# An RNN layer with a gated residual: the input product x Wx issued in two row tiles of 64 partitions in place of the undivided array

## The chip, the cores and the metric

The kernel runs on one core of one Trainium2 chip. The metric is the device time of one execution in microseconds (us), as the median of several runs; lower is better. TensorE's granted clock in the profile of before is 1.000 of full speed.

## The reference, cut to what matters

x is 64 sequences of 256 steps of 1024 numbers, in float32. A first layer adds to x the states of a recurrent network, a second adds a gated copy:

```
N, T, D = 64, 256, 1024
xW = einsum('ntd,dh->nth', x, Wx) + b
for t in range(T):                       # each step needs the one before
    h = tanh(h @ Wh + xW[:, t])          # h starts as cond (64 x 1024)
    out[:, t] = h
x = x + out
gate = sigmoid(silu(cond @ W1.T + b1) @ W2.T + b2)
x = x + inverse_haar(gate * haar(x))     # the gate is one number per sequence and column
```

Since the gate does not depend on the step, the second layer is a multiplication of x by 1 + gate, and the kernel does it so (`factor`).

## The kernel before, in words

The steps are taken in 128 pairs: the 64 sequences of two steps make 128 rows, the tile that TensorE takes as weights. Two products fill the time.

**The product of h, once per step.** h Wh is made in seven products of half the size (Strassen's scheme, `strassen_product`, line 192). Each is 4 blocks times 4 column tiles of 32 (`tile_position=(0, q * R)`, line 204), in plain float32; each matmul is two instructions in the profile, so a product is 32 instructions of line 197. Seven products make a step. Between products ScalarE (ACT) and VectorE (DVE) add, take tanh and transpose; the banks `main0` and `main1` serve here as `m5` and `m7` (line 748).

**The product x Wx, once per pair.** To keep precision with one-pass matmuls (type fp32r), x is split into three parts and Wx too: x0 is the high bits (`high_bits` on DVE, then `cast` on ACT, line 309), x1 the low rest (`low`, line 297), x2 a difference (`difference`, line 302). x2 times the third part of Wx goes into the accumulators `mixed`; x1 and x0 times their parts go into `main`. The 1024 output columns are two halves `h` of 512, one accumulator bank each (`mixed0`, `mixed1`, `main0`, `main1`), and the 1024 of contraction are 8 blocks `k` of 128 rows. So a pair takes 3 x 2 x 8 = 48 matmuls, 128 rows x 128 weight columns, 512 moving columns (`x_matmul`, line 274).

For pairs 7 to 127 these 48 come in `whole` (line 333) in one piece: `mixed` for both halves, then x1 into `main`, then x0. Pairs 1 to 6, in the first twelve steps, use `block`, `first` and `second`.

`take_mixed` (line 317) copies `mixed` out on ACT, half by half, into `sum` and adds the bias on GpSimd (POOL). `finish_half(h)` (line 374) adds `main[h]` to it on DVE. `store` and `reload` (384, 388) carry `sum` through DRAM on SP's queue to the layout of the step, `xw`, which `put_part` (line 611) copies into the accumulators of the coming step.

**Order.** From step 12 on the program orders all engines by hand. Steps go in groups of three (`M = 3`), and after each group comes `beside_x` (line 654): one `whole`, or, where the coming group needs the pair at once (`many`), two with nothing between them on TensorE. In it DVE prepares the next pair's x2 and x1 (`prepare`, line 677) before `finish_half(0)` and `finish_half(1)`; ACT does `take_mixed`, then three `put_part`, then the `cast` of the next pair (line 703, or at the first step of the next group, line 776); POOL multiplies finished x by `factor` (`scale`) and adds the bias. The tiles `high`, `x0`, `x1`, `x2` and `sum` exist once each, and so do the four banks: each is written again only after its last reader.

Of the kernel before, what the change touches and what calls it, by code (L numbers as in the profile page):

```python
# [53 lines left out]
F32 = mybir.dt.float32  # L54
# [7 lines left out]
P = 128  # L62
R = 32
Q = P // R
B = D // P
# [6 lines left out]
M = 3  # L72
NP = T // S
HALF = 512
HIGH = -(1 << 12)
UP = float(1 << 12)
DOWN = 1.0 / UP
# [8 lines left out]
def tile_cond_resid(  # L86
# [14 lines left out]
    nc = tc.nc  # L101
    const = ctx.enter_context(tc.tile_pool(name="const", bufs=1))
# [18 lines left out]
    def high_bits(v, name: str):  # L121
        t = split.tile([P, D], I32, tag="high", name=name)
        nc.vector.tensor_scalar(out=t, in0=v.bitcast(I32), scalar1=HIGH, scalar2=None, op0=ALU.bitwise_and)
        return t[:].bitcast(F32)
# [111 lines left out]
    def put(xw, t: int):  # L236

        acc = bank("acc", f"acc{t}")
        nc.scalar.copy(acc, flat(xw))
        return acc  # L240

    def h_product(acc, a: dict, t: int):

        m16, m57 = (bank(f"m{i}", f"m{i}_{t}") for i in (16, 57))
        m16, m5, m7 = m16[:, :E], m57[:, :E], m57[:, E : 2 * E]
        part = [acc[:, i * E : (i + 1) * E] for i in range(3)]
        y = sums.tile([P, 4, E], F32, tag="y", name=f"y{t}")
        u = sums.tile([P, E], F32, tag="u", name=f"u{t}")
        strassen_product(m16, a[1], 1, True)
        nc.scalar.copy(y[:, 0], m16)  # L250

        strassen_product(part[0], a[2], 2) if t != S else None
        strassen_product(m5, a[5], 5, True)
        strassen_product(m16, a[6], 6)
        nc.scalar.copy(u, m16)
        strassen_product(m7, a[7], 7)
        strassen_product(part[0], a[2], 2) if t == S else None
        if t == 1:
            for k in range(B - 2, B):
                gate_block(k)  # L260
        nc.vector.tensor_add(
            y[:, 1:3], m57[:, : 2 * E].rearrange("p (i e) -> p i e", i=2), u[:].unsqueeze(1).broadcast_to((P, 2, E))
        )
        nc.vector.tensor_add(y[:, 3], m7, y[:, 1])
        strassen_product(part[2], a[4], 4)
        strassen_product(part[1], a[3], 3)
        h = work.tile([P, W], F32, tag="h", bufs=1, name=f"h{t}")
        nc.vector.tensor_add(h, acc, flat(y))
        return h

    def bank(tag: str, name: str):
        return one_pool.tile([P, HALF], F32, tag=tag, name=name)

    def x_matmul(acc, v, which: int, h: int, k: int, start=False, stop=False) -> None:

        nc.tensor.matmul(  # L276
            out=acc[h],
            lhsT=v[:, k * P : (k + 1) * P],
            rhs=wx_s[k][which][:, h * HALF : (h + 1) * HALF],
            start=start and k == 0,  # L280
            stop=stop and k == B - 1,
        )

    class XWork:
# [32 lines left out]
        def take_mixed(self) -> None:  # L317
            self.sum = split.tile([P, D], F32, tag="sum", name=f"sum_{self.i}")
            for h in range(2):
                s = self.sum[:, h * HALF : (h + 1) * HALF]  # L320
                nc.scalar.activation(s, self.mixed[h], AF.Copy, scale=-1.0)  # L321
                nc.gpsimd.tensor_add(s, s, b_row[:, h * HALF : (h + 1) * HALF])  # L322

# [9 lines left out]
        def whole(self) -> None:  # L333

            self.begin()
            for h in range(2):
                for k in range(B):
                    x_matmul(self.mixed, self.x2, 2, h, k, True, True)
            for h in range(2):
                for k in range(B):  # L340
                    x_matmul(self.main, self.x1, 1, h, k, start=True)
            for h in range(2):
                for k in range(B):
                    x_matmul(self.main, self.x0, 0, h, k, stop=True)

        def first(self) -> None:
            self.cast()
# [26 lines left out]
        def finish_half(self, h: int) -> None:  # L374
            v = self.sum[:, h * HALF : (h + 1) * HALF]
            nc.vector.scalar_tensor_tensor(  # L376
                out=v, in0=self.main[h], scalar=1.0 + DOWN, in1=v, op0=ALU.mult, op1=ALU.add
            )
# [40 lines left out]
    wx_s, wh_raw = [], []  # L419
# [15 lines left out]
    acc, acc1, gate_ps = bank("acc", "acc0"), bank("m57", "acc1_raw"), bank("gate", "gate_ps1")  # L435
# [57 lines left out]
    def x_step(t: int):  # L493
        x = pairs[t // S][:].rearrange("p (b s g m) -> p s g b m", b=B, s=S, g=G)
        return x[:, t % S]
# [7 lines left out]
    h = work.tile([P, W], F32, tag="h", bufs=1, name="h0")  # L503
# [4 lines left out]
    for t in range(ALONE):  # L508
# [3 lines left out]
        if t:  # L512
            h = h_product(acc, sides, t)
# [4 lines left out]
        if t == 0:  # L518
            acc = bank("acc", "acc1")
# [18 lines left out]
        elif s == 0:  # L538
            acc = put(xw[1], t + 1)
# [4 lines left out]
        if s == 1 and t + 1 < ALONE:  # L544
            now = later
            now.first()
            acc = put(xw_next[0], t + 1)
# [17 lines left out]
        if LATE <= t < LATE + B:  # L565
            k = t - LATE
# [44 lines left out]
    def put_part(t: int, j: int):  # L611

        part = bank(("acc", "m57", "gate")[j], f"acc{t}_{j}")[:, :E]
        nc.scalar.copy(part, xws[t // S][t % S][:, j])
        return part
# [100 lines left out]
    def kept_step() -> None:  # L716
# [4 lines left out]
        def at(v, n: int):  # L721
            return v[n // S].rearrange("p (b s n) -> p s b n", b=B, s=S)[:, n % S]
# [6 lines left out]
        if not odd:  # L729
# [3 lines left out]
            if n < S * len(kept):  # L733
                again.append(const.tile([P, W], F32, tag="spare", name=f"again{n}"))
                v = again[0][:].rearrange("p (b n) -> p b n", b=B)
                nc.sync.dma_start(out=v, in_=at(kept, n))

    accs = [put_part(ALONE, j) for j in range(3)]
    ends, factors, gaps = [], [], [0]
    later.cast()  # L740
# [2 lines left out]
    for t in range(ALONE, T):  # L743
# [7 lines left out]
        h = work.tile([P, W], F32, tag="h", bufs=1, name=f"h{t}")  # L751
# [35 lines left out]
        elif t > T - 4:  # L787

            v = x_step(t - 1)
# [76 lines left out]
```

## Time and profile before

| | |
|---|---|
| median of 3 runs | 3050.32 us (3049.7 to 3053.82) |
| span of the profiled execution, first to last instruction | 3054.6 us (no other time of this execution is recorded) |
| PE, TensorE's matmuls | 3039.8 us, 63862 instructions |
| PEld, its weight loads | 2716.7 us, 63862 |
| DVE | 1796.3 us |
| ACT | 864.0 us |
| POOL | 772.3 us |
| matmuls of x Wx (line 276) | 4064 into `main`, 2032 into `mixed` |

A line of the page's groups gives source line, engine, operation, output and inputs by the program's names, shapes and count; then busy time in us and the mean of one in ns; then the idle time of the engine before the group and what ended most of it. PE and PEld are two views of TensorE and overlap. Consecutive matmuls overlap as well, so the duration of one is longer than the time from one start to the next; a rate has to be read from starts. In the order of time, a row is a run of equal instructions: start in us, length in us, engine, line, group, count.

### The profile page before, as it was taken

The numbers are of one execution on the slowest core, as the hardware profiler recorded it, in microseconds if no ns is written. First come the engines' busy times: TensorE is split into PE (matmuls) and PEld (weight loads), VectorE is DVE, ScalarE is ACT, GpSimd is POOL, SyncE is SP. The second block draws the span as 40 slices with busy tenths as digits, with TensorE's granted clock in tenths as the row PEclk, the third lists the DMA queues.
The fourth block names the chain that finished last, engine by engine and source line by source line (L and its number), as shares of the span: only waits on it lengthen the run. The fifth ranks groups of instructions, "written<-read, shape, count | busy, mean of one in ns | idle before, by whom it ended". The sixth has DMA issues, their size and how long they took to land.

```text
span 3054.6 us, 141755 instructions
## 1 busy us (share of the span) xinstructions
PE 3039.8 (100%) x63862; PEld 2716.7 (89%) x63862; DVE 1796.3 (59%) x4928; ACT 864.0 (28%) x2641; POOL 772.3 (25%) x521
## 2 busy tenths in 40 slices
PE   9999999999999999999999999999999999999999
PEld 6888998888899988999888889888899988889998
DVE  8555555555555655556555555556556555555555
ACT  3222322222222222222222222222222222222222
POOL 2232222222222222222222222222222222222221
PEclk9999999999999999999999999999999999999999
DMA  7323222333322232222323222223222223332222
GB/s 263 125 98 98 92 92 96 106 103 102 114 91 86 85 100 98 86 86 86 102 96 104 93 86 85 86 88 98 97 86 85 85 97 96 103 100 85 86 85 82
DMA packets 164605, 300.40 MB, mean 98 GB/s; under 512 B 44192, under 2 KB 110496, under 8 KB 164000
## 3 DMA queue, kind: packets, MB, share of 16 engines
q1 hardware_dynamic: 163856, 290.81, 28.6%
q8 instruction: 501, 8.21, 1.1%
q14 instruction: 104, 0.85, 0.1%
q10 hardware_dynamic: 144, 0.52, 0.0%
HBM read 154.93 MB, written 136.31 MB: 95 GB/s over the span
## 4 chain that ended last, share of the span: by engine, by line
PE 99%; issue 0%; POOL 0%; DMA 0%; DVE 0%; SPq 0%; ACT 0%; DVEq 0%
PE main L276 30%; PE acc L197 22%; PE mixed L276 16%; PE m_h L197 14%; PE main_h L197 14%; PE m L197 1%; PE acc L214 0%; PE gate_ps L214 0%; POOL sum L322 0%; DMA wx<-wx 0%; PE acc_raw L214 0%; DVE x L300 0%; SPq L413 0%; ACT sum L321 0%; SPq L119 0%
## 5 line engine op out<-in xcount | busy, mean ns | idle before, releaser
L276 PE MATMUL main<-wx,x 128*128 128x512 f32 x4064 | 945.7, 389 | 0.4 <-DVE x L300 0.4
L276 PEld LDWEIGHTS main<-wx,x 128*128 128x128 f32 x4064 | 762.1, 188 | 161.2 <-issue 2.2
L501 POOL TENSOR_TENSOR x<-x,factor 128x512 f32<-128x512 f32 x242 | 312.0, 1289 | 1318.3 <-DVE x L619 931.5
L322 POOL TENSOR_TENSOR sum<-sum,b_row 128x512 f32<-128x512 f32 x254 | 421.0, 1667 | 849.0 <-ACT sum L321 840.5
L276 PE MATMUL mixed<-wx,x 128*128 128x512 f32 x2032 | 494.7, 395 | 0.0
L276 PEld LDWEIGHTS mixed<-wx,x 128*128 128x128 f32 x2032 | 374.9, 188 | 92.8 <-issue 17.1
L756 ACT ACTIVATE h<-h 128x128 f32<-128x128 f32 x976 | 275.7, 306 | 569.3 <-DVE h L780 376.6
L300 DVE TENSOR_TENSOR x<-x,x_high 128x1024 fp32r<-128x1024 f32 x127 | 178.7, 1407 | 265.5 <-PE main L276 265.5
L760 DVE STREAM_TRANSPOSE hT<-h 128x128 f32<-128x128 f32 x972 | 298.0, 307 | 38.5 <-ACT h L756 38.4
L376 DVE SCALAR_TENSOR_TENSOR sum<-main,sum 128x512 f32<-128x512 f32 x254 | 175.4, 691 | 205.2 <-PE main L276 179.8
L197 PE MATMUL acc<-wh,s 128*32 128x128 f32 x8160 | 283.7, 273 | 2.7 <-issue 2.4
L197 PE MATMUL acc<-wh,hT 128*32 128x128 f32 x8160 | 277.8, 273 | 0.7 <-issue 0.6
L197 PE MATMUL acc<-t,hT 128*32 128x128 f32 x8160 | 276.0, 273 | 1.0 <-issue 0.9
L197 PE MATMUL main_h<-wh,s 128*32 128x128 f32 x7808 | 269.9, 273 | 1.3 <-issue 1.1
L197 PE MATMUL main_h<-t,s 128*32 128x128 f32 x7808 | 269.9, 273 | 1.2 <-issue 0.9
L197 PE MATMUL m_h<-t,s 128*32 128x128 f32 x7808 | 269.7, 273 | 0.8 <-issue 0.6
L197 PE MATMUL m_h<-wh,hT 128*32 128x128 f32 x7808 | 263.7, 274 | 0.2
L305 DVE SCALAR_TENSOR_TENSOR x<-x_high,x 128x1024 fp32r<-128x1024 f32 x127 | 178.8, 1408 | 133.5 <-PE mixed L276 133.4
L321 ACT ACTIVATE sum<-mixed 128x512 f32<-128x512 f32 x254 | 146.9, 598 | 366.3 <-DMA sum_d<-sum 186.6
L197 PEld LDWEIGHTS acc<-wh,s 128*32 128x32 f32 x8160 | 237.5, 110 | 7.0 <-issue 7.0
L197 PEld LDWEIGHTS m_h<-wh,hT 128*32 128x32 f32 x7808 | 213.8, 110 | 30.1 <-issue 29.5
L197 PEld LDWEIGHTS acc<-wh,hT 128*32 128x32 f32 x8160 | 234.0, 110 | 3.7 <-issue 2.6
(81 smaller groups left out, 2751.3 us busy)
## 6 DMA issues: line engine op xcount, KB each, us to landing
x<-xT SPq DMA_DIRECT2D x127, 512.0 KB, 4.6
sum_d<-sum SPq DMA_DIRECT2D x127, 512.0 KB, 3.1
xw<-sum_d SPq DMA_DIRECT2D x1016, 64.0 KB, 2.0
yT<-x SPq DMA_DIRECT2D x122, 512.0 KB, 2.8
wh<-wh SPq DMA_DIRECT2D x8, 512.0 KB, 11.0
w<-w1T SPq DMA_DIRECT2D x8, 512.0 KB, 8.7
w<-w2T SPq DMA_DIRECT2D x8, 512.0 KB, 4.4
wx<-wx SPq DMA_DIRECT2D x7, 512.0 KB, 8.5
```

The costliest lines, as they stand in the source:

```text
L197: nc.tensor.matmul(out=out[q * R : (q + 1) * R], lhsT=a[:, k * R : (k + 1) * R], rhs=wh_s.sides[i][k][:, q], start=first and k == 0, stop= ...
L276: nc.tensor.matmul(out=acc[h], lhsT=v[:, k * P : (k + 1) * P], rhs=wx_s[k][which][:, h * HALF : (h + 1) * HALF], start=start and k == 0, s ...
L300: nc.vector.tensor_sub(self.x1, x, self.high)
L305: nc.vector.scalar_tensor_tensor(out=self.x2, in0=self.high, scalar=1.0 + DOWN, in1=pairs[i], op0=ALU.mult, op1=ALU.subtract)
L321: nc.scalar.activation(s, self.mixed[h], AF.Copy, scale=-1.0)
L322: nc.gpsimd.tensor_add(s, s, b_row[:, h * HALF : (h + 1) * HALF])
L376: nc.vector.scalar_tensor_tensor(out=v, in0=self.main[h], scalar=1.0 + DOWN, in1=v, op0=ALU.mult, op1=ALU.add)
L501: nc.gpsimd.tensor_mul(of_step(x, s), of_step(x, s), blocks(factor))
L756: nc.scalar.activation(quad(h, j), quad(h, j), AF.Tanh)
L760: nc.vector.transpose(quad(hT, j), quad(h, j))
```

## The change

`whole` issues the same sums in another cut. A matmul no longer covers the 128 rows of block k; it covers 64, and two such matmuls, one for the upper and one for the lower 64 rows (`r`), are issued one after the other at `tile_position=(0, 0)` and `(64, 0)`. At any time the two write different banks: in the first three passes (`turned = 0`; x2, x1, x0) row tile 0 works for half 0 and row tile 1 for half 1; in the last three, halves are exchanged, so that each bank has received both row tiles' parts at the end. A pass is 8 blocks x 2 = 16 matmuls with 512 moving columns; six passes make 96 matmuls with their weight loads where there were 48. After the first and the third pass ACT copies one element of `mixed[1]` or `main[1]` into a spare tile `turn`; the next write of row tile 0 into that bank, two passes or one pass later, waits for this reader.

```
         def whole(self) -> None:
 
             self.begin()
-            for h in range(2):
-                for k in range(B):
-                    x_matmul(self.mixed, self.x2, 2, h, k, True, True)
-            for h in range(2):
-                for k in range(B):
-                    x_matmul(self.main, self.x1, 1, h, k, start=True)
-            for h in range(2):
-                for k in range(B):
-                    x_matmul(self.main, self.x0, 0, h, k, stop=True)
+            for turned in range(2):
+                for acc, v, which in ((self.mixed, self.x2, 2), (self.main, self.x1, 1), (self.main, self.x0, 0)):
+                    for k in range(B):
+                        for r in range(2):
+                            h = r ^ turned
+                            rows = slice(r * HP, (r + 1) * HP)
+                            nc.tensor.matmul(
+                                out=acc[h],
+                                lhsT=v[rows, k * P : (k + 1) * P],
+                                rhs=wx_s[k][which][rows, h * HALF : (h + 1) * HALF],
+                                start=not turned and k == 0 and which > 0,
+                                stop=turned == 1 and k == B - 1 and which != 1,
+                                skip_group_check=True,
+                                tile_position=(r * HP, 0),
+                            )
+                    if not turned and which != 1:
+                        nc.scalar.copy(turn, acc[1][:1, :1])
...
+    turn = const.tile([1, 1], F32, tag="turn", name="turn")
```

`HP` is 64. Nothing else is changed; the other users of `x_matmul` stay.

More of the change, by code (lines that the diff above doesn't have):

```diff
@@ L74 @@
 HALF = 512
+HP = P // 2
 HIGH = -(1 << 12)
```

## The prediction

> **What bounds the kernel now.** I read the page from the chain of work downwards, since it says whose time the end is made of, then the costliest groups, then the order of time in one stage.
>
> ```profile
> span 3054.6 us, 141755 instructions
> ...
> PE 3039.8 (100%) x63862; PEld 2716.7 (89%) x63862; DVE 1796.3 (59%) x4928; ACT 864.0 (28%) x2641; POOL 772.3 (25%) x521
> ...
> PE 99%; issue 0%; POOL 0%; DMA 0%; DVE 0%; SPq 0%; ACT 0%; DVEq 0%
> ...
> L276 PE MATMUL main<-wx,x 128*128 128x512 f32 x4064 | 945.7, 389 | 0.4 <-DVE x L300 0.4
> L276 PEld LDWEIGHTS main<-wx,x 128*128 128x128 f32 x4064 | 762.1, 188 | 161.2 <-issue 2.2
> ...
> L276 PE MATMUL mixed<-wx,x 128*128 128x512 f32 x2032 | 494.7, 395 | 0.0
> ...
> L197 PEld LDWEIGHTS acc<-wh,s 128*32 128x32 f32 x8160 | 237.5, 110 | 7.0 <-issue 7.0
> ```
>
> The chain is TensorE and nothing else. The 6096 matmuls of x Wx (4064 + 2032, 48 for each of 127 pairs) keep it busy for 1440 us. Their idle time before is 0.4 us, so they wait for nobody. What an edit does here it does through the time between matmul starts. A weight load of 128 columns is shown as 188 ns, one of 32 columns (the products of h) as 110.
>
> The durations overlap, so a rate is read from starts. Next view: TensorE in order of time, over two pairs that follow each other (the stage in which `whole` runs twice) and the first products of h behind them. Columns: start us, duration of the merged run, then the group and its count.
>
> ```profile
> 1030.39 3.92 PE L276 MATMUL mixed<-wx,x 128*128 128x512 f32 x16
> 1034.15 7.42 PE L276 MATMUL main<-wx,x 128*128 128x512 f32 x32
> 1041.41 3.79 PE L276 MATMUL mixed<-wx,x 128*128 128x512 f32 x16
> 1045.04 7.42 PE L276 MATMUL main<-wx,x 128*128 128x512 f32 x32
> 1052.38 1.08 PE L197 MATMUL m_h<-wh,hT 128*32 128x128 f32 x32
> 1053.28 1.06 PE L197 MATMUL acc<-t,hT 128*32 128x128 f32 x32
> 1054.15 1.06 PE L197 MATMUL acc<-wh,hT 128*32 128x128 f32 x32
> ```
>
> From 1034.15 to 1041.41, 32 matmuls take 7.26 us: **226.9 ns each**; the 16 from 1041.41 take 3.63, again 226.9. The first 16 take 3.76, so entering from the products of h costs 0.13 us. A product of h, 32 instructions in four column tiles side by side, takes 0.87 us (1053.28 to 1054.15; 0.873 over the six that follow): 218.3 ns for eight. The start of the kernel has column tiles with 256 moving columns:
>
> ```profile
> 21.30 1.05 PE L214 MATMUL acc_raw<-wx,x 128*32 128x256 f32 x16
> 22.17 1.05 PE L214 MATMUL acc<-wx,x 128*32 128x256 f32 x16
> 23.03 1.05 PE L214 MATMUL acc_raw<-wx,x 128*32 128x256 f32 x16
> 23.89 7.09 PE L214 MATMUL acc<-wh,h0T 128*32 128x256 f32 x128
> ```
>
> 48 in 2.59 us: four side by side take **215.8 ns**. Their mean duration (379 to 413 by tile) is near the 389 of an x matmul, so one instruction of theirs is about as long as one of L276, yet a round of them returns in 216 where the undivided array needs 227. So 11 ns of each x matmul are a gap which rows with tiles side by side do not have.
>
> **The change, part by part.** *Matmuls.* In each of 121 `whole` calls (pairs 7 to 127; the first six go through `block`, `first` and `second`, untouched) 48 matmuls of 128 rows become 48 couples of 64 rows, with the same 512 columns and 128 weight columns per member. That makes 5808 couples, and 5808 more matmuls and weight loads. Each ns of couple time P is worth 5.81 us. No row shows row tiles. Bounds: P = 215.8 (the column tiles' round) gives (226.9 − 215.8) × 5.81 = −64.5 us; P = 453.8 (members one after the other) +1318 us. Between ends so far apart I go by the nearest rows, those with tiles side by side: 215.8 and, with twice as many weight columns in a round (8 × 32 = 256, just what a couple loads), 218.3. I take the middle, 217.1: 9.8 × 5.81 = **−56.9 us**.
>
> *Weight loads.* They double: 256 columns per couple instead of 128. In a product of h 256 columns are loaded in 218.3 ns beside the matmuls, so this load rate is shown to hide; 188 − 110 = 78 ns for 96 more columns is 0.81 ns per column, 208 for 256, also under 217. If the cover is gone, the second rival follows. The Trainium skill speaks against the change here (TensorE: Matmul & The Clock Gate, "LDWEIGHTS (loading the stationary operand)"): load time goes by columns, columns / 1.2 ns, and fewer rows save nothing. The row's slope (0.81) agrees; by the page a couple's loads make an estimated 213 ns, 4 under my P, and the sum would stand. The same page ("Wait — 56ns, not 53.3ns?") gives 215.7 ns from start to start for 512 columns once warm; the measured 226.9 disagrees, and by the page there would be no gap to win on the undivided array.
>
> *Entering and leaving.* `beside_x` runs 81 times (40 with two `whole`, 41 with one: 121). Entering costs 0.13 now; the first couple must load twice, at most 109 ns more (half of 218), or the entry could vanish. Bounds −10.5 to +8.8 us; I take half a load: **+4.4 us**.
>
> *Turn copies.* 242 ACT copies of one element. The smallest PSUM copies of the trace, 128x128, take 0.26 to 0.27 us (the `u` and `acc` copies), so at most 65 us on an engine that is 28% busy. TensorE waits for them: pass 4 for a copy of the end of pass 1, pass 5 for one of the end of pass 3. Slack: two passes (3.5 us) and one (1.7 us) against 0.2 us release and 0.27 us copy. Ahead of the copy on ACT stand tanh and `cast` (1.06), done 1.2 us into the second `whole`. Cost 0; behind the copies wait `take_mixed`, which is later anyway.
>
> *What moves.* `mixed` ends after pass 4, not after the first third; `main0` and `main1` end together at the end. The first `whole`, from its start, passes of 8 × 0.2171 = 1.74: ends at 1.87, 3.60, 5.34, 7.08, 8.81, 10.55. These rows of the same stage (all engines in order of time) price what follows:
>
> ```profile
> 1034.35 1.50 DVE L305 SCALAR_TENSOR_TENSOR x<-x_high,x 128x1024 fp32r<-128x1024 f32 x1 [0.73 <-PE mixed L276]
> ...
> 1039.85 0.69 DVE L376 SCALAR_TENSOR_TENSOR sum<-main,sum 128x512 f32<-128x512 f32 x1 [0.52 <-PE main L276]
> ...
> 1041.68 0.69 DVE L376 SCALAR_TENSOR_TENSOR sum<-main,sum 128x512 f32<-128x512 f32 x1 [1.13 <-PE main L276]
> ...
> 1045.12 1.09 ACT L321 ACTIVATE sum<-mixed 128x512 f32<-128x512 f32 x2 [2.46 <-DMA sum_d<-sum]
> ...
> 1045.80 3.06 POOL L322 TENSOR_TENSOR sum<-sum,b_row 128x512 f32<-128x512 f32 x2 [7.55 <-ACT sum L321]
> ```
>
> With 0.2 us of release (in this stage ACT starts 2.15 us in, on eight matmuls streamed by 1.95): ACT takes `mixed` 7.3 to 8.5; POOL adds from 8.0 for 3.06 (3.60 in another stage) to 11.0–11.6; on DVE the next x2 7.3 to 8.8, x1 9.0 to 10.4, then `finish_half(0)` 10.75 to 11.45 and `finish_half(1)` to 12.15–12.3. The second `whole` needs x2 at 10.55, x1 at 12.3, x0 (cast 10.75 to 11.8) at 14.0, and **both main banks at 12.3**, where they had over 2 us before. That is the one new edge: 0 to 0.2 us in 40 stages, 0 to +8 us, I take 0.05: **+2 us**. SP's store of `sum` moves 0.7 us later against the end of the first `whole`, and behind it on SP stand a `yT` store and eight reloads, whose `xw` is read after the second `whole`, 10 us on. The wait of ACT for that store (2.46 above) goes, off the path. Towards products of h, `m5` and `m7` need the main banks 2.6 and 4.4 us after the end; they are free at 1.0 and 1.7.
>
> *Sum.* −56.9 + 4.4 + 2 = −50.5: a span of 3054.6 becomes 3004. No time but the span is recorded for the profiled execution; it stands 0.14% above the median of the runs, 3050.32, so the forecast in their measure is **3000 us**.
>
> **Rivals.** *The gap belongs to each tile.* All rows without it have 32 weight columns, the one with it 128, and a row tile keeps 128. Then P = 226.9: 0, plus entry and edge, 0 to +16.8: 3050 to 3067. For it: that distinction. Against: nothing but the analogy with tiles.
>
> *The two weight loads queue, slower.* Place: the load path between members. It decides once two loads cost over 226.9, 113.5 each. With loads in series at half a products' round (109.2 each, 218.3) and the array's gap of 11.1 (226.9 − 215.8) once per couple, P = 229.4: +14.5 + 6.4, **3071**; with the gap behind each load 240.5, +79 + 6.4, 3136; with the shown 188 in series 376, +866, 3920. Against it: in the products the 110 ns loads follow at 27 ns.
>
> *The members do not run side by side at all*, so the change does not do what it says: 226.9 per member, +1318, 4370. Against: column tiles do, for four.
>
> *A wait replaces the gap*: main banks or a turn copy late by over 1.3 us in each double stage would eat the gain (54 / 40); the slack above speaks against.
>
> **Chances.** Forecast 0.50; own gap 0.22; queueing loads up to 3136 0.14; loads or members in full series 0.12; new wait 0.02. The range reaches from the best bounds (−64.5 − 10.5: 2975) to 3100, the middle of the queueing case; outside remain its upper half, full series and what is worse than the bounds, under 0.2. The forecast's own range is 2975 to 3020. A measurement here can tell 0.2% (6 us) from no change. Faster 0.50; same 0.12 (the lower half of the own-gap case); slower 0.38.
>
> **What would show it.** Row-tile matmuls of `mixed` and `main` whose 16 per pass of 1.74 us start in couples; a `whole` of 10.4 to 10.6 us instead of 10.97 and 11.02; weight loads still 188 with starts 109 apart on average; idle before `main` under 8 us in all. A pass of 1.82 means that the gap is the tile's; 1.84 or more, that loads queue; 3.6, that members alternate. Idle on `main` released by DVE `sum` or ACT `turn` would show the wait.

## The result, and the profile after

The changed kernel takes 3066.95 us (median of 4 runs, 3064.56 to 3068.51) beside 3051.56 us of the kernel before: a ratio of 1.0048, 95% interval 1.0034 to 1.0062. It is slower by about 15 us (10 to 19); the prediction said 50 us faster. Run again beside other runs of before, as `rows_again` below, it gave 1.0053 (1.0040 to 1.0065).

The page of the changed kernel, the lines that answer to those of before:

```profile
span 3065.1 us, 153573 instructions
...
L343 PE MATMUL main<-wx,x 64*128 64x512 f32 x7744 | 939.8, 387 | 0.0
L343 PEld LDWEIGHTS main<-wx,x 64*128 64x128 f32 x7744 | 749.3, 184 | 149.0 <-DVE sum L385 8.5
L323 POOL TENSOR_TENSOR sum<-sum,b_row 128x512 f32<-128x512 f32 x254 | 494.0, 1965 | 1149.9 <-ACT sum L322 1059.3
```

Twice as many matmuls, each about as long as before (387 ns against 389), are busy for about the same time: the two members of a couple do lie side by side. A couple of 64 rows costs what one matmul of 128 rows cost. Two things are new: weight loads into `main` waited 8.5 us in all for DVE's `sum`, and POOL's additions went from 1667 to 1965 ns.

TensorE in order of time, over a double stage and the first product of h behind it:

```profile
1032.96 2.11 PE L343 MATMUL mixed<-wx,x 64*128 64x512 f32 x16
1034.90 3.79 PE L343 MATMUL main<-wx,x 64*128 64x512 f32 x32
...
1043.97 1.98 PE L343 MATMUL mixed<-wx,x 64*128 64x512 f32 x16
1045.79 3.86 PE L343 MATMUL main<-wx,x 64*128 64x512 f32 x31
...
1055.24 1.08 PE L198 MATMUL m_h<-wh,hT 128*32 128x128 f32 x32
```

A pass (16 matmuls in 8 couples) from 1043.97 to 1045.79 takes 1.82 us: **227 ns per couple**, the 226.9 of the undivided array. In the trace the two members start 3 to 4 ns apart, and so do their weight loads; then nothing starts for 223. The double stage took 21.99 us before (1030.39 to 1052.38); here it takes 22.28. Over all stages with x Wx after 200 us, from the starts in both traces: 41 single stages 11.111 us before and 11.115 after; 39 double stages 22.00 before and **22.30** after. So 0.30 us in each of 40 double stages, 12 us, is what the change costs there, and nothing else in these stages moved.

Where the 0.30 arises: all engines in order of time at the seam of the two `whole` calls.

```profile
1041.22 3.94 POOL L323 TENSOR_TENSOR sum<-sum,b_row 128x512 f32<-128x512 f32 x2 [10.33 <-ACT sum L322]
...
1042.36 1.64 DVE L301 TENSOR_TENSOR x<-x,x_high 128x1024 fp32r<-128x1024 f32 x1 [0.59 <-PE main L343]
...
1044.23 0.69 DVE L385 SCALAR_TENSOR_TENSOR sum<-main,sum 128x512 f32<-128x512 f32 x1 [0.23 <-PE main L343]
...
1045.20 0.69 DVE L385 SCALAR_TENSOR_TENSOR sum<-main,sum 128x512 f32<-128x512 f32 x1 [0.28 <-POOL sum L323]
...
1045.95 3.27 PEld L343 LDWEIGHTS main<-wx,x 64*128 64x128 f32 x30 [0.20 <-DVE sum L385]
```

Read it backwards. The second `whole` wants main1 at 1045.79. The weight load of row tile 1 was held until 1045.95, after the second `finish_half` (1045.20 to 1045.89). That one had sat idle 0.28 us for POOL's second addition, which ended at 1045.16: the two additions took 3.94 us, beside DVE's making of x1, itself 1.64 us. By then the earlier matmul of row tile 1, under which its load hides elsewhere, was over, so the next matmul of row tile 1 starts at 1046.28 instead of 1046.01. Of these 0.27 us, 0.16 are the wait beyond 1045.79; the other 0.11 are, as far as the trace tells, part of the weight load (0.18 us), which no longer hides in full.

### The profile page after: what moved, and what is told of

Read it like the earlier page. It is cut to its first block, busy times and chain, and to the rows that moved or that the text cites. A ratio compares the mean times of both kernels' runs of the same rounds, so it can differ in the third digit from the quotient of the medians.

```text
span 3065.1 us, 153573 instructions
## 1 busy us (share of the span) xinstructions
PE 3047.6 (99%) x69670; PEld 2734.8 (89%) x69670; DVE 1817.0 (59%) x4928; ACT 886.2 (29%) x2883; POOL 834.4 (27%) x521
## 4 chain that ended last, share of the span: by engine, by line
PE 99%; issue 0%; POOL 0%; DMA 0%; DVE 0%; SPq 0%; ACT 0%; DVEq 0%
PE main L343 29%; PE acc L198 22%; PE mixed L343 15%; PE m_h L198 14%; PE main_h L198 14%; PE main L277 1%; PE m L198 1%; PE mixed L277 1%; PE acc L215 0%; PE gate_ps L215 0%; POOL sum L323 0%; DMA wx<-wx 0%; PE acc_raw L215 0%; DVE x L301 0%; SPq L422 0%
## 5 line engine op out<-in xcount | busy, mean ns | idle before, releaser
L343 PE MATMUL main<-wx,x 64*128 64x512 f32 x7744 | 939.8, 387 | 0.0
L343 PEld LDWEIGHTS main<-wx,x 64*128 64x128 f32 x7744 | 749.3, 184 | 149.0 <-DVE sum L385 8.5
L323 POOL TENSOR_TENSOR sum<-sum,b_row 128x512 f32<-128x512 f32 x254 | 494.0, 1965 | 1149.9 <-ACT sum L322 1059.3
L343 PE MATMUL mixed<-wx,x 64*128 64x512 f32 x3872 | 499.8, 392 | 0.0
L306 DVE SCALAR_TENSOR_TENSOR x<-x_high,x 128x1024 fp32r<-128x1024 f32 x127 | 156.6, 1233 | 541.0 <-PE mixed L343 541.0
L343 PEld LDWEIGHTS mixed<-wx,x 64*128 64x128 f32 x3872 | 369.1, 184 | 83.7 <-issue 16.1
L301 DVE TENSOR_TENSOR x<-x,x_high 128x1024 fp32r<-128x1024 f32 x127 | 206.9, 1629 | 70.6 <-PE main L343 70.6
L198 PEld LDWEIGHTS acc<-t,hT 128*32 128x32 f32 x8160 | 232.0, 110 | 3.3 <-issue 2.7
L198 PEld LDWEIGHTS m_h<-t,s 128*32 128x32 f32 x7808 | 225.8, 110 | 4.1 <-issue 3.9
```

The lines of the kernel that those rows point to most:

```text
L198: nc.tensor.matmul(out=out[q * R : (q + 1) * R], lhsT=a[:, k * R : (k + 1) * R], rhs=wh_s.sides[i][k][:, q], start=first and k == 0, stop= ...
L301: nc.vector.tensor_sub(self.x1, x, self.high)
L306: nc.vector.scalar_tensor_tensor(out=self.x2, in0=self.high, scalar=1.0 + DOWN, in1=pairs[i], op0=ALU.mult, op1=ALU.subtract)
L343: nc.tensor.matmul(out=acc[h], lhsT=v[rows, k * P : (k + 1) * P], rhs=wx_s[k][which][rows, h * HALF : (h + 1) * HALF], start=not turned an ...
```

## The experiments

The edits are shown abridged, with comments added. Distances between starts are medians over a trace where no rows are named.

**What I held after the result.** Theory: the gap per matmul is each row tile's own, so nothing is won, and the 15 us are mainly the wait at the seam. Rivals: the doubled instructions and loads cost a little everywhere; and for the gap, that it goes with weight columns, with the type, or with the undivided array.

### `rows_first`: row tiles only in the first `whole`

```
             if many:
                 now = nxt
                 now.cast()
-                now.whole()
+                now.undivided()      # the `whole` of the kernel before
```

> Row tiles in every first `whole`, the undivided form in the second `whole` of the 40 double stages. Theory (the gap of 11 ns is each tile's own, so couples cost what single matmuls cost; the added time is the wait for the main banks at the second `whole`, 0.30 us in each of 40 double stages = 12 us): couples still 226.9 ns, single stages 11.11 us, double stages back from 22.30 to 22.00 us, the median within 0.15% of before. Rival (doubled instructions and weight loads cost a little everywhere): 81 of 121 pairs keep it, so two thirds of the 15 us remain, a ratio of about 1.0033.

Measured: 3069.03 us against 3056.06 before, ratio 1.0042 (1.0029 to 1.0055). Single stages 11.11, double stages 22.25 us. Neither the double stages nor the median came as the theory said, though no load waits for `sum` any longer. The loss sits elsewhere:

```profile
1041.80 3.79 PE L343 MATMUL main<-wx,x 64*128 64x512 f32 x32
1045.52 3.94 PE L277 MATMUL mixed<-wx,x 128*128 128x512 f32 x16
1049.30 7.42 PE L277 MATMUL main<-wx,x 128*128 128x512 f32 x32
```

The 32 row-tile matmuls take 3.72 us where two passes take 3.63, and the first 16 undivided ones 3.78 where 16 take 3.63: the change of tile form inside the stage costs 0.24 us, nearly as much as the wait that it removes. With it 40 more weight loads into `mixed` stand idle for about 0.35 us, released by nothing that the profile shows (14.9 us in 44 cases, against 0.8 in 4 in the changed kernel). The experiment traded one cost for the other. The rival's ratio of 1.0033 lies within the interval, but its account does not hold: the 41 single stages, all in row tiles, took no longer than before.

### `rows_nobias`: the seam without POOL

```
                 nc.scalar.activation(s, self.mixed[h], AF.Copy, scale=-1.0)
-                nc.gpsimd.tensor_add(s, s, b_row[:, h * HALF : (h + 1) * HALF])
```

> The changed kernel without POOL's addition of the bias to `sum` in `take_mixed` (the bias is left out). Theory A (the chain at the edge runs over POOL: its two additions took 3.9 us in place of 3.1 beside DVE's making of x1, and `finish_half(1)` waited for the second): main1 is free about 0.3 us sooner, 1.6 us after the first `whole` against a pass of 1.8, so double stages return to 22.00 to 22.05 us and the ratio to before is within 0.1%; x1's subtraction falls from 1.63 to about 1.23 us. Theory B (the two `finish_half` in a row behind the end fill the pass by themselves): double stages stay at 22.2 to 22.3, ratio 1.003 to 1.005.

```profile
L301 DVE TENSOR_TENSOR x<-x,x_high 128x1024 fp32r<-128x1024 f32 x127 | 155.5, 1224 | 70.5 <-PE main L342 70.5
```

Measured: ratio 1.0011 (1.0002 to 1.0019); double stages 22.04 us; no load waits for `sum`; x1's subtraction 1.22 us. That is theory A, with the ratio just beyond its 0.1%: the chain ran over POOL. The two `finish_half` alone fit into the pass.

### `rows_spare`: another bank at the seam

```
-            self.main = [bank(f"main{h}", ...) for h in range(2)]
+            self.main = [bank("m16" if spare and h else f"main{h}", ...) for h in range(2)]
...
-        now.whole()
+        now.whole(many)          # spare = many: the first `whole` of a double stage
```

> The changed kernel, with the bank of `m16`, unused between groups, in place of main1 in the first `whole` of a double stage, so that the second `whole` has no reader of main1 to wait for. All of the computation is kept, and no tiling mode changes inside a stage. Theory (the cost of the change is the wait at that bank): double stages return from 22.30 to 22.00 us, no wait on `main` for DVE's `sum`, 12 us less than the changed kernel, ratio to before 0.999 to 1.002. Rival (the wait is only where a general slowing shows up): double stages stay above 22.2 and the ratio near 1.004.

```profile
1030.33 2.11 PE L343 MATMUL mixed<-wx,x 64*128 64x512 f32 x16
...
1041.34 1.98 PE L343 MATMUL mixed<-wx,x 64*128 64x512 f32 x16
...
1052.31 1.08 PE L198 MATMUL m_h<-wh,hT 128*32 128x128 f32 x32
```

The second `whole` takes 10.97 us here (1041.34 to 1052.31), as in the kernel before (1041.41 to 1052.38). Measured: 3058.36 us against 3056.29 before, ratio 1.0008 (0.9999 to 1.0017), and 11 us less than `rows_again` beside it. Double stages 22.00 us. POOL's additions are still at 1957 ns, but nobody on TensorE waits for them. So the wait at main1 is the cost of the change in these stages, and without it row tiles come out neither better nor worse than the undivided array, within 0.2%.

### `rows_again`: the changed kernel once more

> The changed kernel once more, on the chip and beside the runs of before that `rows_spare` has. Both theories: ratio 1.003 to 1.006, double stages 22.30 us.

Measured: 3069.73 us, ratio 1.0053 (1.0040 to 1.0065), double stages 22.30 us, as expected.

### `short256`: half the moving columns

```
+        for c in range(0, HALF, 256):
             nc.tensor.matmul(
-                out=acc[h],
+                out=acc[h][:, c : c + 256],
...
-                rhs=wx_s[k][which][:, h * HALF : (h + 1) * HALF],
+                rhs=wx_s[k][which][:, h * HALF + c : h * HALF + c + 256],
```

> The undivided form with each matmul cut into two of 256 moving columns and the same 128 weight columns (all of the sum is computed). If the gap is a fixed time per matmul: 215.8 / 2 + 11.1 = 119 ns from start to start, a pair 11.4 us in place of 10.9, some +65 us in all. If the weight load (188 ns as shown) or its hand-over sets the distance between starts: 188 to 227 ns, a pair 18 to 22 us, +850 to +1320 us. If the gap goes with the moving data's length: 113 ns, no change.

```profile
1053.94 7.84 PE L287 MATMUL main<-wx,x 128*128 128x256 f32 x64
1061.62 4.00 PE L287 MATMUL mixed<-wx,x 128*128 128x256 f32 x32
```

Measured: 7.68 us for 64 matmuls, 120 ns from start to start (so in 11126 of 11535 cases of the trace); 3129.25 us in one run (+73). Taken as a + b per column, 226.9 − 120 = 106.9 ns for 256 columns make b 0.418 ns, and **a is 13 ns at both lengths**. That the time is a straight line in the columns is assumed; two lengths cannot test it. The weight load, still 188 ns as shown, does not set the distance.

### `narrow`: fewer weight columns

```
+    out=acc[h][:columns],                    # columns: 32 for half 0, 64 for half 1
+    lhsT=v[:, k * P : k * P + columns],      # x0 pass, blocks 0 to 6
```

> The undivided form, in which seven of eight matmuls of each half of the x0 pass have fewer weight columns: 32 for half 0, 64 for half 1 (the other 96 or 64 output rows of these blocks are left out). Theory (the gap goes with the 128 weight columns of a tile): starts 216 ns apart with 32 columns, between 216 and 227 with 64. Rival (the gap belongs to one-pass fp32r matmuls with 512 moving columns, whatever the weights): 226.9 in both.

```profile
1039.93 1.78 PE L286 MATMUL main<-wx,x 128*32 128x512 f32 x7
1041.55 0.40 PE L276 MATMUL main<-wx,x 128*128 128x512 f32 x1
1041.79 1.78 PE L286 MATMUL main<-wx,x 128*64 128x512 f32 x7
1043.40 0.39 PE L276 MATMUL main<-wx,x 128*128 128x512 f32 x1
```

Seven starts take 1.62 us with 32 columns and 1.61 with 64: 231 and 230 ns. The gap does not shrink with the weights. This ends the reason that I had given for the rival that came true.

### `types`: three types on the undivided array

```
+    x_typed(high_half, self.mixed, self.x2, ...)                  # x2: 16 upper bits, as bf16
+    x_typed(lambda v: v.bitcast(F32), self.main, self.x1, ...)    # x1: plain float32
     x_matmul(self.main, self.x0, 0, h, k, stop=True)
```

> The undivided form with other types of the same tiles: the x2 pass reads the upper 16 bits of its operands as bf16 (the lower bits are left out), the x1 pass takes plain float32, the x0 pass stays fp32r. Theory C (the 13 ns that a 512-column and a 256-column matmul have alike belong to fp32r): bf16 starts 216 ns apart; plain float32, two instructions of 427 ns streaming by the products' rate, 429 to 432 ns apart each. Theory D (they belong to any matmul of the undivided array and to any row tile of 128 weight columns, and only column tiles lack them): bf16 227, plain float32 440.

```profile
1415.07 13.89 PE L289 MATMUL main<-wx,x 128*128 128x512 f32 x32
```

Measured, in starts: bf16 225, plain float32 429 per instruction (13.89 us less the 0.592 of the last one, over 31 distances). Neither theory as written: the bf16 of C (216) and the float32 of D (440) both failed. By the 0.418 ns per column of `short256`, 1024 columns' time for a plain float32 instruction (two passes) is 428: a gap of 1 to 2 ns on the undivided array with 128 weight columns. So plain float32 has next to no gap, on the undivided array as in the column tiles of the products, and both kinds of one-pass matmuls tried so far have it. The bf16 operands here lay in steps of two, four bytes apart, which left a question.

### `rows_types`: plain float32 in row tiles

```
-    lhsT=v[rows, k * P : (k + 1) * P],
+    lhsT=as_type(v[rows, k * P : (k + 1) * P], which),    # which == 1: bitcast(F32); rhs alike
```

> The changed kernel with the x1 passes in plain float32 and the x2 and x0 passes in fp32r as they were, all in row tiles. `types` gave 429 ns for plain float32 and 225 to 227 for one-pass matmuls on the undivided array. Theory E (the 13 ns are of one-pass matmuls, divided or not; a plain float32 matmul has 2 to 3): couples of the x1 passes 429 ns per instruction, the fp32r ones 226.9. Rival (row tiles add a gap of their own): 440 in the x1 passes. The longer stage also hides the wait for the main banks less or more, so only starts are read.

```profile
1405.36 8.85 PE L346 MATMUL main<-wx,x 64*128 64x512 f32 x48
1414.05 1.98 PE L346 MATMUL mixed<-wx,x 64*128 64x512 f32 x16
```

Measured: row tile by row tile, plain float32 instructions start 429 ns after their predecessors, the fp32r ones 227. The row shows both: per row tile, 16 float32 instructions and 8 fp32r matmuls, 16 x 429 + 8 x 227 = 8.68 us, and 8.69 from 1405.36 to 1414.05. Row tiles neither add a gap nor take one away.

### `dense16` and `stepped16`: the spacing of the moving data

```
+    rhs=dense[:, :HALF],                 # dense16: 512 bf16 next to each other
+    rhs=high_half(b_row[:, :HALF]),      # stepped16: 512 bf16, four bytes apart
```

> The undivided form, the x2 pass with moving data and weights dense in bf16, the x1 pass with dense bf16 moving data and weights of 16 bits in steps of two, the x0 pass in fp32r as before (operands of x2 and x1 are replaced by the bias row read as bf16, so their products are left out). Theory E (every one-pass matmul has the gap): 225 to 227 ns in both passes. Rival (the gap comes with reading moving data at four bytes per column and cycle, which fp32r and the stepped bf16 of `types` share): 216 ns in both. If only the weights' spacing counts: 216 in the x2 pass, 225 in the x1 pass.

> As `dense16`, with the same values (the bias row, read as bf16, in place of the operands of the x2 and x1 passes), but the moving data taken in steps of two, so four bytes apart. Theory F (moving data at four bytes per column bring the gap): 225 to 227 ns from start to start in both passes, a double stage 1.0 us longer than that of `dense16` (3 x 32 matmuls less the x0 ones, 64 x 11 ns x 2 = 1.4 us at most). Rival (in `dense16` the values, which are the bias, made the difference): 216 ns.

`dense16`, then `stepped16`, a first `whole` (of the 16 matmuls of each `mixed` row the trace of `dense16` records 15):

```profile
1015.89 3.40 PE L289 MATMUL mixed<-b_row 128*128 128x512 bf16 x15 [0.16 <-issue]
1019.13 3.62 PE L289 MATMUL main<-b_row,x 128*128 128x512 bf16 x16
1022.39 4.03 PE L276 MATMUL main<-wx,x 128*128 128x512 f32 x16
```

```profile
1026.94 3.79 PE L289 MATMUL mixed<-b_row 128*128 128x512 bf16 x16
1030.57 3.76 PE L289 MATMUL main<-b_row,x 128*128 128x512 bf16 x16
1033.97 4.00 PE L276 MATMUL main<-wx,x 128*128 128x512 f32 x16
```

Between neighbouring starts of line 289 the median is **216 ns in `dense16` and 225 in `stepped16`**, with operands from the same bias row (the dense ones take in the lower halves of its numbers too). In the rows it is read from their lengths, less one matmul, over 15 distances: 3.62 − 0.38 gives 216, 3.76 − 0.39 gives 225. The start of the row behind does not serve here, since the first fp32r matmul is recorded as starting 0.03 us after the last bf16 one. The fp32r pass keeps its 227 in both runs. The device times of single runs agree: `dense16` lies 47 us under the run of before beside it, `stepped16` 12, where 3872 matmuls at 11 and 2 ns less make 43 and 8. (The 1.4 us at most of the second expectation count the 64 matmuls of a double stage twice; 64 x 11 ns is 0.7.) In both runs, the weights of the second pass are stepped, which makes no difference. So the gap comes with moving data that lie four bytes apart and are streamed in one pass. Stepped bf16 and fp32r have that in common; why it costs a time per matmul no run shows.

## Why the prediction was wrong

**The step that failed is the choice of P.** I took the rows "nearest" to row tiles to be those "with tiles side by side" (215.8 and 218.3) and priced the gap of 11 ns at −56.9 us. Measured: P = 227 and 0 us. Those rows differ from the x matmuls in more than one way: they are in column tiles, they have 32 weight columns, and they are plain float32. I read the first difference as the cause, gave the second to a rival and never weighed the third, though my own description said "in plain float32; each matmul is two instructions" of one product and "type fp32r" of the other. There was a sign: the 215.8 ns are for 256 moving columns, the 226.9 for 512, and I did not ask why half the columns take as long. `types` shows plain float32 with next to no gap on the undivided array too, and `rows_types` shows fp32r with it in row tiles: between these forms the type decides, and row tiles change nothing. fp32r in column tiles was not run.

**The rival that came true, for another reason.** "The gap belongs to each tile" gave P = 226.9 and 3050 to 3067, and the time lies at its upper end. That is luck: of its 16.8 us 8.8 were for entering, which cost nothing, and 8 for the main banks, which cost 12. Its argument, that a row tile keeps 128 weight columns, is refuted by `narrow` (231 ns with 32 columns).

**Weight loads.** Right: doubled loads hide. The members' loads start 3 ns apart and the couple still returns in 227; a load of 64 rows is shown as 184 ns, one of 128 rows as 188. The rivals on queueing loads and on members one after the other did not occur.

**Entering and leaving.** Forecast +4.4; single stages went from 11.111 to 11.115, which is nothing. The second first load goes beside the first.

**Turn copies.** Right at 0: 242 copies of 0.15 us each, and no instruction waited for one.

**The main banks at the second `whole`.** The edge and its place were forecast, at 0 to 0.2 us per stage and +2 us in all; measured 0.30 and 12 us. Before, the second `finish_half` ended at 1042.37 and the second `whole` first wrote main1 eight matmuls after 1045.04, at about 1046.86: 4.5 us of slack. The chain was right link by link, and two sizes were off. POOL's two additions, which I took at 3.06 to 3.60 from stages where x1's subtraction starts only when they have ended, took 3.94 beside it (they ended 12.2 us into the first `whole`, forecast 11.0 to 11.6); and a wait in front of a weight load costs part of the load as well, 0.11 us.

**The sum.** With the measured terms it reads 0 + 0 + 12. The profiled spans differ by 10.5 (3065.1 − 3054.6), the medians by 15.4. The few us between are not located: `rows_spare` and `rows_nobias`, with double stages at 22.00 and 22.04, still stand 2 and 4 us above before, the first within its interval of no change, the second just outside it. Span less stages is 1741.0 us before and 1739.6 after, and 1738.5 to 1746.8 in `rows_spare`, `rows_nobias`, `rows_again`, `rows_first` and `short256`: a few us come and go outside the stages without the change. `short256` has as many TensorE instructions as the changed kernel, and its 73 us are matched by its stages (1386.0 against 1313.6 us in all), so the instruction count by itself costs about nothing.

The 215.7 ns from start to start for 512 columns that the Trainium skill gives (TensorE: Matmul & The Clock Gate, "Wait — 56ns, not 53.3ns?") are met here by dense bf16 (216) and missed by fp32r and stepped bf16 (227 and 225). So that figure, which the prediction set aside, was a hint that the undivided array need not have the gap. The Trainium skill also states that changing the tiling mode drains TensorE (TensorEngine Tiling (Array Packing), "Key Properties"); `rows_first` agrees, with 0.24 us for a change inside the stage.

**No version that computes the whole sum beats the kernel before.** `rows_spare` mends the seam and comes out at no difference. Whether column tiles, the form of the rows that misled me, would free fp32r of its gap stays open.

## What to carry to other kernels

A gap between matmuls has to be pinned to one of its conditions before a change is built on it: of two rows that differ in tile form and in type, either may explain it, and one run with a single condition changed (here plain float32 on the undivided array) separates them. Splitting a matmul into row tiles that stream the same columns won nothing here, where TensorE was already fed. When accumulators finish together at the end of a piece rather than one after the other, look at who writes them next: slack of 4.5 us here became none, and every link behind it (ACT, POOL, DVE) then counts.

## What the runs showed of the hardware that I had not expected

- One-pass matmuls with moving data four bytes apart cost 13 ns (fp32r, 227 for 512 columns, 120 for 256) or 11 ns (stepped bf16, 225 against the same 214 for 512 columns) beyond 0.418 ns per column; dense bf16 (216) and plain float32 (429 for what that rate makes two passes of 512 columns) cost 1 to 2.
- Two row tiles of 64 work fully side by side, weight loads included: four instructions where there were two, in the same 227 ns.
- POOL's addition of two 128x512 operands and DVE's subtraction of two 128x1024 operands slow each other when they meet: from before to after the means went from 1667 to 1965 ns on POOL and from 1407 to 1629 on DVE; without the addition the subtraction takes 1224 (`rows_nobias`).
- Going from 64-row tiles to the undivided array inside a stage costs 0.24 us.
